# Layer 0 selective scan: VectorE runs product, product, scan, scan in each quarter

## The chip, the core and the metric

The kernel runs on one core of one Trainium2 chip, in one launch. The metric is the device time of one execution in microseconds (us), lower is better. Five engines run side by side, each with its own in-order queue: PE (TensorE, matmuls), DVE (VectorE), ACT (ScalarE), POOL (GpSimd) and SP (SyncE, which only issues DMAs here). They meet through semaphores.

## What is computed

Two "metaformer" layers over an image batch of 2 x 96 channels x 96 x 96. Layer 0 is a Mamba-like block: a 3x3 convolution gives sampling offsets, the sampled image is cut into windows, and every window is run through a selective scan in four directions with 16 states. Then come a layer norm, a gate, a projection and a small quantized MLP. Layer 1 is an attention block with an MLP. The change is in the scan of layer 0:

```
def step(hst, inputs):
    ut, dt, bt, ct = inputs
    dA = jnp.exp(dt[..., None] * A)
    hst = hst * dA + (dt * ut)[..., None] * bt[:, :, None, :]
    y = jnp.einsum('bkdn,bkn->bkd', hst, ct)
    return (hst, y)
```

So the scan needs, for each channel, state and time step, a decay `dA`, an input `dt*u*b`, a linear recurrence over time, a product with `c`, and a sum over the states.

## The kernel before

**Tiling.** Layer 0 works stripe by stripe: 2 images x 16 stripes of 6 rows (576 tokens). A stripe goes through three stages, which overlap with those of its neighbours: the front (`_l0_front`: norm, input projection, the 3x3 convolution `pc` at L551, the sampling, the scan's inputs), the scan (`_l0_scan`, L951) and the back (`_l0_back`: norm, gate, projection, MLP). While stripe n is scanned, the front of a later stripe and the back of an earlier one run beside it.

**The scan.** `_l0_scan` loops over 2 channel halves h, 2 orders o and 2 directions kk; each of these 8 sections (`_l0_section`, L992) loops over 4 groups of states, the quarters i (`quarter`, L1017), and each quarter over 2 token halves c (`unit`, L1034). A stripe is thus 32 quarters or 64 units, and the kernel has 1024 quarters or 2048 units. A tile of a unit is 128 partitions x 864 fp32. One quarter makes its decays on ACT, three instructions into one tile `dA` for both units (L1025). One unit u is then this chain:

- the spread (L1040, PE): a matmul copies the 288 values of b to 128 partitions, in PSUM tile `bp`;
- the product (L1044, DVE): `dur * bp`, in place over 864 columns of `bp`;
- the scan (L1060, DVE): the recurrence over `dA` and `bp`, into tile `h`;
- times_c (L1065, POOL): `h *= cre`;
- the states (L1077, PE): three or six matmuls fold the 16 states into the PSUM tile `y`, which gathers 32 units.

**Buffers.** `bp` has 2 buffers (the spread of unit u+2 has to wait for the scan of unit u), `dA` has 2 (the decays of quarter q+2 wait for the last scan of quarter q), `h` has 6 (the scan of unit u+6 needs the states of unit u to be done).

**Waits put on the product.** In a unit with c = 0 the product also carries the waits that the scans of the quarter would have: for the decays, and for times_c and the states of unit u-5 (`wait` at L998, called at L1050).

**What sets the order.** Nothing above is issued in the order of the loops. Every operation is recorded in a `_Plan` with an engine, a cost in us, the tiles it reads and writes and a due time. `order` (L142) then plays a list scheduler over all of layer 0: each engine takes, among the operations that could start first, the one with the earliest due time. A result is taken to reach another engine `LAG` us after its producer ends (L99: 1.5 for DVE, 1.0 for POOL, 0.6 for ACT, 0.5 for PE), and the same engine `SAME` = 0.06 us after. The list sorted by planned start is issued, and `_in_order` (L56) pins each engine to it. On the chip only this order remains, not the planned times: an engine takes its next instruction when its semaphores allow. Due times: the spread of a unit is due 60 tau before the unit (tau = 3.4 us), so that it goes first whenever it can; product and scan are due 30 tau after it, in the order product, scan, product, scan.

Of the kernel before, what the change touches and what calls it, by code (L numbers as in the profile page):

```python
# [13 lines left out]
ALU = mybir.AluOpType  # L14
# [14 lines left out]
WIN = 6  # L29
# [3 lines left out]
H2 = T // 2  # L33
NS = 16
KG = 4
NQ = 4
CB = 32
NBL = C // CB
# [50 lines left out]
class _Op:  # L89
    def __init__(self, eng, cost, run, due, tab):  # L90
        self.eng, self.cost, self.run, self.due, self.tab = eng, cost, run, due, tab
        self.deps, self.tiles, self.start, self.end = set(), [], None, None
        self.left, self.then, self.ready = 0, [], 0.0

SAME = 0.06
LAG = {"pe": 0.5, "dve": 1.5, "act": 0.6, "pool": 1.0, "sp": 1.5}  # L99


class _Plan:
# [39 lines left out]
    def order(self):  # L142

        free = {e: 0.0 for e in ("pe", "dve", "act", "pool", "sp")}
        ready = {e: [] for e in free}
        tab, wire = None, 0.0
        for n, o in enumerate(self.ops):
            o.no = n
            o.left = len(o.deps)
            for p in o.deps:  # L150
                p.then.append(o)
        for o in self.ops:
            if not o.left:
                ready[o.eng].append(o)
        left, out = {id(t): len(t.users) for o in self.ops for t in o.tiles}, []
        while len(out) < len(self.ops):
            best = None
            for e, queue in ready.items():
                pick = None
                for o in queue:  # L160
                    at = max(free[e], o.ready)
                    for t in o.tiles:
                        if t.slot is None:
                            s = t.place()
                            if s is None:
# [12 lines left out]
                if pick and (best is None or pick[1] < best[1]):  # L178
                    best = pick
            assert best, "the plan is stuck"  # L180
            _, at, o = best
            ready[o.eng].remove(o)
            cost = o.cost
            if o.tab is not None and o.tab != tab:
                tab, cost = o.tab, cost + 1.3
            for t in o.tiles:
                if t.slot is None:
                    t.slot = t.place()
                    t.slot[0] = t
                    if t.tag != "p":  # L190
                        t.queue.pop(0)
            o.start = at
            if o.eng == "sp":
                free["sp"] = at + 0.6
                wire = max(wire, at + 1.0) + cost
                o.end = wire + 2.0
            else:
                o.end = free[o.eng] = at + cost
            for p in o.then:
                p.left -= 1  # L200
                p.ready = max(p.ready, o.end + (SAME if p.eng == o.eng else LAG[p.eng]))
# [781 lines left out]
HEAD = 14 * SEQ  # L983


def _tail(py, b):

    n = T - HEAD
    return py.ap[NBL * CB :, b * n : b * n + n]


def _l0_section(k, P, S, f, first, o, h, kk, py, at, tau):  # L992


# [20 lines left out]
    dlr, dur = reps  # L1015
# [18 lines left out]
    def unit(u, i, c, cre, dA, t0):  # L1034
        toks = slice(c * H2, (c + 1) * H2)
        bp = S.tile(P.ps, [128, 1024], "bp", 2)
        ht = S.tile(P.rep, [128, NBL, H2], "h", P.nh)

        def spread():
            nc.tensor.matmul(  # L1040
                bp.ap[:, :H2], k.selb[:, kk, i, :], f.bc[o].ap[:, toks], start=True, stop=True)

        def product():
            nc.vector.tensor_tensor(  # L1044
                bp.ap[:, : NBL * H2].rearrange("p (b n) -> p b n", b=NBL)[:, ::-1],
                dur.ap[:, ::-1, toks],
                bp.ap[:, :H2].unsqueeze(1).to_broadcast([128, NBL, H2]), ALU.mult)
# [7 lines left out]
        def scan():  # L1055
            hv, dv = (v.rearrange("p b n -> p (b n)") for v in (ht.ap, dA.ap[:, c]))
            bv = bp.ap[:, : NBL * H2]
            if kk:
                hv, dv, bv = hv[:, ::-1], dv[:, ::-1], bv[:, ::-1]
            nc.vector.tensor_tensor_scan(hv, dv, bv, 0.0, ALU.mult, ALU.add)  # L1060

        S.op("dve", 2.0, scan, (dA, bp), (ht,), due=t0 + (1.35 - P.early["dve"]) * tau)

        def times_c():
            nc.gpsimd.tensor_tensor(  # L1065
                ht.ap, ht.ap, cre.ap[:, toks].unsqueeze(1).to_broadcast([128, NBL, H2]), ALU.mult)
            P.issued["pool", u] = latest()

        S.op("pool", 2.06, times_c, (cre,), (ht,), due=t0 + (2.3 - P.early["pool"]) * tau)

        def states():
            end = o == 1 and kk == 1 and i == NQ - 1

            def part(dst, v, stop):
                if o:
                    v = v.rearrange("p (w j i) -> p w i j", i=WIN, j=WIN)
                nc.tensor.matmul(dst, k.fold, v, start=False, stop=stop)  # L1077

            for blk in range(NBL):
                dst = py.ap[CB * blk : CB * blk + CB]  # L1080
                n = HEAD - H2 if c else H2
                part(dst[:, c * H2 : c * H2 + n], ht.ap[:, blk, :n], end and c == 1)
            if c:
                for blk in range(NBL):
                    part(_tail(py, blk), ht.ap[:, blk, n:], end and blk == NBL - 1)
            P.issued["pe", u] = latest()

        S.op("pe", 1.0, states, (ht,), (py,), due=t0 + (3.5 - P.early["pe"]) * tau)

    for i in range(NQ):  # L1090
        quarter(i)
# [2 lines left out]
def _layer0(k, tc, a, x, x2d):  # L1094


    nc = k.nc
    with ExitStack() as st:
        P = Ctx()
        pool = lambda name, bufs, **kw: st.enter_context(tc.tile_pool(name=name, bufs=bufs, **kw))  # L1100
# [747 lines left out]
def tile_metaformer(ctx: ExitStack, tc: tile.TileContext, a, out):  # L1848
# [100 lines left out]
```

## Time and profile before

| what | value |
|---|---|
| time, median of 3 runs (lowest, highest) | 8538.53 us (8529.44, 8542.10) |
| the profiled execution: time, span in the trace | 8525.04 us, 8523.3 us |
| layer 0 up to its last scan | 0 to about 6475 us of the span |
| busy share of the span: PE, DVE, ACT, POOL | 86%, 92%, 74%, 71% |
| one product, one scan (DVE) | 1044 ns, 1953 ns, x2048 each |
| one times_c (POOL) | 2027 ns, x2048 |
| mean granted TensorE clock | 0.911 |

The profile page gives, for one profiled execution, each engine's busy time, the costliest groups of instructions (line, engine, operation, output <- input, shapes, count, then busy us, mean ns of one, and idle us of the engine just before them with what ended most of it) and the chain of work that ended last. Queries of the same trace give the waits (who waited for whom), a timeline in order of time, and the busy time of each engine in chosen windows. A window's row reads: from:to, length, then busy us of PE, PEld (weight loads), DVE, ACT and POOL with the number of instructions, then granted clock, DMA share and GB/s.

### The profile page before, as it was taken

The page shows a single profiled execution, that of the slowest core. Times are in us where ns is not written, and L with a number is a line of the kernel's source. Part 1 is how long each engine was busy: PE and PEld are TensorE (multiplying, and loading weights), DVE is VectorE, ACT ScalarE, POOL GpSimd, SP SyncE. Part 2 cuts the span into 40 slices and gives each one's busy share as a digit, 9 for nine tenths or more (in the row PEclk, how much of TensorE's full clock was granted, in tenths as well). Part 3 has the DMA queues.
Part 4 walks back from the last instruction along what each step waited for, and adds up shares of the span by engine and source line. Part 5 has one row for each costly group of instructions (what it writes and reads, how often), then busy time and mean ns, then how long its engine had stood idle before and what let it go on. Part 6 is the DMA issues. An engine that isn't in the chain of part 4 may idle for free. (4 is left out here: it accounts for less than half of the span.)

```text
span 8523.3 us, 118902 instructions
## 1 busy us (share of the span) xinstructions
PE 7295.1 (86%) x43653; PEld 3402.1 (40%) x43653; DVE 7815.6 (92%) x5398; ACT 6339.3 (74%) x10688; POOL 6026.9 (71%) x3835
## 2 busy tenths in 40 slices
PE   7888888888888888888888888888866999989998
PEld 4443444444443444444444444443423223542245
DVE  3899999999999999999999999999996998959988
ACT  5777777777777777777777777777755886778867
POOL 4999999999999999999999999999984000110001
PEclk8899999999989888988999998989867999989999
DMA  2444444444444444444444444444442000110001
GB/s 89 141 153 148 150 152 147 148 151 144 149 146 144 151 146 152 149 150 153 146 150 151 146 145 151 146 151 150 146 143 76 3 2 14 34 48 3 2 21 32
DMA packets 339992, 985.62 MB, mean 116 GB/s; under 512 B 50152, under 2 KB 51872, under 8 KB 339104
## 3 DMA queue, kind: packets, MB, share of 16 engines
q1 hardware_dynamic: 337488, 977.74, 36.8%
q8 instruction: 347, 5.69, 0.3%
q14 instruction: 253, 2.07, 0.1%
q10 hardware_dynamic: 1904, 0.12, 0.0%
HBM read 797.19 MB, written 139.25 MB: 110 GB/s over the span
## 5 line engine op out<-in xcount | busy, mean ns | idle before, releaser
L1065 POOL TENSOR_TENSOR h<-h,cre 128x864 f32<-128x864 f32 x2048 | 4121.2, 2027 | 428.2 <-DVE h L1060 277.3
L1060 DVE TENSOR_TENSOR_SCAN h<-dA,bp 128x864 f32<-128x864 f32 x2048 | 3996.6, 1953 | 105.5 <-PE y L1077 25.5
L1025 ACT ACTIVATE dA<-dlr,A 128x576 f32<-128x576 f32 x3072 | 2155.9, 765 | 815.3 <-DVE h L1060 758.5
L1044 DVE TENSOR_TENSOR bp<-dur,bp 128x864 f32<-128x864 f32 x2048 | 2135.5, 1044 | 201.8 <-PE bp L1040 80.4
L1077 PE MATMUL y<-h,fold 128*32 128x288 f32 (+2 forms) x18432 | 1856.8, 449 | 465.3 <-POOL h L1065 444.4
L551 PE MATMUL pc<-xin,off 96*96 96x288 f32 x4608 | 1331.7, 421 | 0.1
L1077 PEld LDWEIGHTS y<-h,fold 128*32 128x32 f32 x18432 | 756.1, 117 | 1245.1 <-POOL h L1065 809.6
L1413 ACT ACTIVATE pr<-sc 128x960 f32<-128x960 f32 (+1 forms) x1080 | 954.1, 937 | 201.7 <-PE sc L1409 181.5
L1040 PE MATMUL bp<-bt,selb 128*128 128x288 bf16 x2048 | 640.9, 314 | 516.9 <-DVE h L1060 506.5
L1493 DVE TENSOR_TENSOR sums<-sums,pr 128x3840 f32<-128x3840 f32 (+1 forms) x240 | 959.0, 3996 | 56.7 <-ACT pr L1413 34.4
L1585 POOL MEMSET vch<- 96x32 f32 x16 | 2.4, 153 | 1298.1 <-DVE dist L1447 1208.1
L551 PEld LDWEIGHTS pc<-xin,off 96*96 96x96 f32 x4608 | 705.9, 165 | 505.9 <-issue 236.8
L1040 PEld LDWEIGHTS <-selb 128*128 128x128 bf16 x2048 | 201.5, 99 | 1204.1 <-DVE h L1060 930.4
L1409 PE MATMUL sc<-qH,kH 32*128 32x480 f32 (+1 forms) x3240 | 627.1, 602 | 10.1 <-DMA q<-qH 5.1
L1409 PE MATMUL sc<-q,kH 32*128 32x480 f32 (+1 forms) x1080 | 564.6, 602 | 0.0
L1475 PE MATMUL av<-pr,vT 128*32 128x480 f32 (+1 forms) x4320 | 533.2, 564 | 3.7 <-ACT av L1500 3.5
L1666 DVE SCALAR_TENSOR_TENSOR acc<-vch,lepe_w,acc 96x1152 f32<-96x1152 f32 x320 | 469.2, 1466 | 8.2 <-ACT vch L1601 0.4
L867 POOL TENSOR_TENSOR x<-x,fy 96x576 f32<-96x576 f32 x32 | 55.0, 1719 | 479.5 <-ACT fy L866 415.4
L1409 PEld LDWEIGHTS sc<-qH,kH 32*128 32x128 f32 x3240 | 218.9, 184 | 419.1 <-issue 219.9
L724 PE MATMUL pt<-xd,w_dt 96*128 96x288 f32 x768 | 290.5, 474 | 15.1 <-ACT xin L516 7.2
L743 POOL TENSOR_TENSOR e<-e,du 128x576 f32<-128x576 f32 x192 | 272.6, 1420 | 31.4 <-ACT du L739 30.9
L746 POOL TENSOR_TENSOR du<-dl,x 128x576 f32<-128x576 f32 x192 | 271.5, 1414 | 6.6
(270 smaller groups left out, 10018.1 us busy)
## 6 DMA issues: line engine op xcount, KB each, us to landing
cre<-c_d SPq DMA_DIRECT2D x1024, 288.0 KB
dur<-du_d SPq DMA_DIRECT2D x256, 864.0 KB
dlr<-dl_d SPq DMA_DIRECT2D x256, 864.0 KB
x<-xs SPq DMA_DIRECT2D x512, 72.0 KB
du_d<-du SPq DMA_DIRECT2D x128, 288.0 KB
dl_d<-dl SPq DMA_DIRECT2D x128, 288.0 KB
du_d<-du SPq DMA_DIRECT2D x128, 144.0 KB
dl_d<-dl SPq DMA_DIRECT2D x128, 144.0 KB
```

Of the source, the lines that this page charges most:

```text
L551: pe(H2, lambda: nc.tensor.matmul(pc.ap[:C, :H2], k.w_c1[:, ih, tap, oh * C : (oh + 1) * C], xin.ap[:, ih, 3 * c + dy : 3 * c + dy + 3, dx ...
L1025: nc.scalar.activation(dA.ap[:, :, blk, :], dlr.ap[:, blk, :].rearrange("p (c n) -> p c n", c=2), AF.Exp, scale=k.A[:, i, kg, h, blk : blk ...
L1040: nc.tensor.matmul(bp.ap[:, :H2], k.selb[:, kk, i, :], f.bc[o].ap[:, toks], start=True, stop=True)
L1044: nc.vector.tensor_tensor(bp.ap[:, : NBL * H2].rearrange("p (b n) -> p b n", b=NBL)[:, ::-1], dur.ap[:, ::-1, toks], bp.ap[:, :H2].unsquee ...
L1060: nc.vector.tensor_tensor_scan(hv, dv, bv, 0.0, ALU.mult, ALU.add)
L1065: nc.gpsimd.tensor_tensor(ht.ap, ht.ap, cre.ap[:, toks].unsqueeze(1).to_broadcast([128, NBL, H2]), ALU.mult)
L1077: nc.tensor.matmul(dst, k.fold, v, start=False, stop=stop)
L1409: nc.tensor.matmul(two[to // 2][:, to % 2, :n], kH[rows, k0 : k0 + 128], q, start=True, stop=True)
L1413: nc.scalar.activation(pr[:, 2 * i : 2 * i + 2, :n], two[i][:, :, :n], AF.Exp, scale=HD**-0.5)
L1475: nc.tensor.matmul((main if s < HEADS else other)[s * HD : (s + 1) * HD, :n], vT[:, blk, hd, :], pr[:, place(s, p), :n], start=at == 0, st ...
L1493: nc.vector.tensor_tensor(both, both, pr[:, :, :, :n], ALU.add)
L1666: S.op("dve", 1.43, lambda: nc.vector.scalar_tensor_tensor(acc.ap, src(), W.lw[:, t : t + 1], acc.ap, ALU.mult, ALU.add), (vch,), (acc,))
```

## The change

The spread, product, scan, times_c and states of a unit stay as they are, and so do all tiles and buffers. Four things differ:

- `rest` (scan, times_c, states) of the first unit of a quarter is recorded only after the product of the second. A pseudo tile `P.turn` is written by every product and scan, which makes the planner keep them in the order of recording: product 0, product 1, scan 0, scan 1, then the next quarter. Other VectorE work may still be planned between them.
- The planner takes the spread's result to reach VectorE 0.6 us after its end (`SOON`) instead of 1.5 us. Every other operation keeps `LAG`.
- The planner's cost of a product is 1.0 us instead of 1.03.
- Due times are the same.

```diff
@@ class _Op
-        self.left, self.then, self.ready = 0, [], 0.0
+        self.left, self.then, self.ready, self.lag = 0, [], 0.0, LAG
...
 SAME = 0.06
+SOON = {"dve": 0.6}
 LAG = {"pe": 0.5, "dve": 1.5, "act": 0.6, "pool": 1.0, "sp": 1.5}
@@ order
-                p.ready = max(p.ready, o.end + (SAME if p.eng == o.eng else LAG[p.eng]))
+                p.ready = max(p.ready, o.end + (SAME if p.eng == o.eng else o.lag[p.eng]))
@@ unit
-        S.op("pe", 0.3, spread, (f.bc[o],), (bp,), due=t0 - P.early["pe"] * tau)
-        S.op("dve", 1.03, product, (dur,), (bp,), due=t0 - P.early["dve"] * tau)
+        S.op("pe", 0.3, spread, (f.bc[o],), (bp,), due=t0 - P.early["pe"] * tau).lag = SOON
+        S.op("dve", 1.0, product, (dur,), (bp, P.turn), due=t0 - P.early["dve"] * tau)
+
+        def rest():
...
-        S.op("dve", 2.0, scan, (dA, bp), (ht,), due=t0 + (1.35 - P.early["dve"]) * tau)
+            S.op("dve", 2.0, scan, (dA, bp), (ht, P.turn), due=t0 + (1.35 - P.early["dve"]) * tau)
...
+        if c == 0:
+            P.behind = rest
+        else:
+            P.behind()
+            rest()
@@ _layer0
         S, tau = _Plan(k), 3.4
+        P.turn, P.behind = S.held(k.ident, "turn"), None
```

More of the change, by code (lines that the diff above doesn't have):

```diff
@@ L1050, in product @@
                 wait([("act", u), ("pool", free), ("pe", free)])
-        S.op("pe", 0.3, spread, (f.bc[o],), (bp,), due=t0 - P.early["pe"] * tau)
-        S.op("dve", 1.03, product, (dur,), (bp,), due=t0 - P.early["dve"] * tau)
[L1055 to L1060, printed above, removed]
@@ L1062, in unit @@
-        S.op("dve", 2.0, scan, (dA, bp), (ht,), due=t0 + (1.35 - P.early["dve"]) * tau)
[L1064 to L1083, printed above, removed]
-                for blk in range(NBL):
-                    part(_tail(py, blk), ht.ap[:, blk, n:], end and blk == NBL - 1)
-            P.issued["pe", u] = latest()
@@ L1088, in unit, with scan, times_c, states @@
-        S.op("pe", 1.0, states, (ht,), (py,), due=t0 + (3.5 - P.early["pe"]) * tau)
+        S.op("pe", 0.3, spread, (f.bc[o],), (bp,), due=t0 - P.early["pe"] * tau).lag = SOON
+        S.op("dve", 1.0, product, (dur,), (bp, P.turn), due=t0 - P.early["dve"] * tau)
+        def rest():
+            def scan():
+                hv, dv = (v.rearrange("p b n -> p (b n)") for v in (ht.ap, dA.ap[:, c]))
+                bv = bp.ap[:, : NBL * H2]
+                if kk:
+                    hv, dv, bv = hv[:, ::-1], dv[:, ::-1], bv[:, ::-1]
+                nc.vector.tensor_tensor_scan(hv, dv, bv, 0.0, ALU.mult, ALU.add)
+            S.op("dve", 2.0, scan, (dA, bp), (ht, P.turn), due=t0 + (1.35 - P.early["dve"]) * tau)
+            def times_c():
+                nc.gpsimd.tensor_tensor(
+                    ht.ap, ht.ap, cre.ap[:, toks].unsqueeze(1).to_broadcast([128, NBL, H2]), ALU.mult)
+                P.issued["pool", u] = latest()
+            S.op("pool", 2.06, times_c, (cre,), (ht,), due=t0 + (2.3 - P.early["pool"]) * tau)
+            def states():
+                end = o == 1 and kk == 1 and i == NQ - 1
+                def part(dst, v, stop):
+                    if o:
+                        v = v.rearrange("p (w j i) -> p w i j", i=WIN, j=WIN)
+                    nc.tensor.matmul(dst, k.fold, v, start=False, stop=stop)
+                for blk in range(NBL):
+                    dst = py.ap[CB * blk : CB * blk + CB]
+                    n = HEAD - H2 if c else H2
+                    part(dst[:, c * H2 : c * H2 + n], ht.ap[:, blk, :n], end and c == 1)
+                if c:
+                    for blk in range(NBL):
+                        part(_tail(py, blk), ht.ap[:, blk, n:], end and blk == NBL - 1)
+                P.issued["pe", u] = latest()
+            S.op("pe", 1.0, states, (ht,), (py,), due=t0 + (3.5 - P.early["pe"]) * tau)
```

## The prediction

> **What bounds the kernel now.** I read the page's busy shares first, then the busy time by window, then the timeline of VectorE, then its waits. The scan stage (250 to 6475 us), then the four eighths of one stripe's scan (eight quarters each) further in:
>
> ```profile
> 250.00:6475.00 6225.00, 5182.08 (x30861) 2518.45 (x30859) 5969.35 (x4217) 4659.94 (x8046) 5764.36 (x3555) 0.90 0.47 147
> ...
> 1149.00:1202.00 53.00, 41.30 (x235) 20.27 (x233) 48.05 (x34) 36.25 (x72) 51.01 (x31) 0.77 0.44 131
> 1202.00:1251.00 49.00, 36.99 (x219) 17.32 (x220) 47.29 (x35) 43.42 (x79) 47.22 (x30) 0.93 0.51 160
> 1251.00:1299.00 48.00, 40.78 (x267) 20.31 (x266) 47.52 (x35) 39.40 (x68) 47.73 (x33) 0.93 0.52 163
> 1299.00:1346.00 47.00, 45.23 (x267) 22.89 (x266) 46.46 (x33) 30.67 (x43) 37.82 (x22) 1.00 0.48 143
> ```
>
> VectorE (fifth number) is busy 96% of the stage: it is the bound. But POOL (seventh) stands at 93%, and not evenly: full in the first three windows, idle for 9 us in the fourth. There the convolution fills PE (third number), 45.2 of 47 us. So a faster VectorE soon meets POOL in one part of a stripe and PE in another. The pattern repeats every 197 us, the time of a stripe.
>
> ```profile
> 2549.81 1.95 DVE L1060 TENSOR_TENSOR_SCAN h<-dA,bp 128x864 f32<-128x864 f32 x1
> 2552.10 2.03 DVE L1044 TENSOR_TENSOR bp<-dur,bp 128x864 f32<-128x864 f32 x2 [0.34 <-PE bp L1040]
> 2554.04 3.79 DVE L1060 TENSOR_TENSOR_SCAN h<-dA,bp 128x864 f32<-128x864 f32 x2
> 2557.80 1.06 DVE L1044 TENSOR_TENSOR bp<-dur,bp 128x864 f32<-128x864 f32 x1
> 2558.90 1.95 DVE L1060 TENSOR_TENSOR_SCAN h<-dA,bp 128x864 f32<-128x864 f32 x1
> 2560.77 1.04 DVE L1044 TENSOR_TENSOR bp<-dur,bp 128x864 f32<-128x864 f32 x1
> 2561.84 1.95 DVE L1060 TENSOR_TENSOR_SCAN h<-dA,bp 128x864 f32<-128x864 f32 x1
> ```
>
> The old order already has a few pairs. Two products and two scans took 5.70 us to the next product (2552.10 to 2557.80). In the usual order a scan starts 1.07 us after its product, and the next product 1.87 us after that scan, so a quarter is 5.89.
>
> ```profile
> DVE bp L1044 <- PE bp L1040: 80.1, 79, 3.3
> DVE bp L1044 <- PE y L1077: 48.6, 30, 3.1
> DVE h L1060 <- PE y L1077: 21.7, 11, 3.6
> DVE bp L1044 <- POOL h L1065: 9.9, 22, 0.8
> ```
>
> VectorE's waits in the stage (total us, times, longest) are about 180 us, 5.7 per stripe. A stripe now is 32 x 5.89 = 188.5, plus 3.2 of other VectorE work, plus 5.6 of waits: 197.3, as seen.
>
> **Part 1, the gain.** Over all records of the stage, start to start, medians: product to its own scan 1076 ns, scan to product 1870; in the pairs product to product 949 to 972 (32 cases), scan to scan 1863 (37), and a product to a scan that is not its own about 960. A quarter goes from 2 x (1076 + 1870) = 5.89 to 960 + 960 + 1863 + 1870 = 5.65 us: 0.24 less, 7.6 per stripe, some 235 us for the 990 quarters not yet paired. The built order confirms that all 1024 quarters become product, product, scan, scan (52 groups now). What it removes is the exposed time in which a scan waits for its own product's write.
>
> The Trainium skill, "VectorE: DVE Perf Modes", section "The DRAIN you can't avoid", says that a semaphore between chained VectorE operations costs nothing and that the gap can't be skipped. By it this term would be 0, and the forecast 235 us later. The rows (1076 against 960) speak against it here, and I go by them.
>
> **Part 2, the spread loses its cover.** A spread needs the `bp` that a scan frees. From the records: scan end to weight load 0.05 us, matmul start to product start 0.33, so 0.39 at least. Before, a whole unit lay between (2.9 us). After, the spread for the first product of a quarter has the other scan (1.87), slack 1.5 us; that for the second has one product (0.96), slack 0.57. A spread behind one or two convolution matmuls (0.52 each) is just in time. In the old trace 38% of the spreads end more than 0.57 us later than they could, 18% more than 1.47, with mean excess over all spreads of 0.42 and 0.17 us.
>
> **Part 3, POOL's lead.** The built order of PE decides how late POOL may be, since PE waits for times_c in `states` and the next spread queues behind it. Before, the spread of unit j mostly stands behind the states of unit j-4, in a stripe's first part of j-5 to j-7. After, that of each quarter's first unit stands behind the states of j-3, nearly without exception. So: scan 2 of a quarter ends; its times_c ends 2.2 us later at best (POOL does the first scan's before); the states need 0.9, the spread and its way to VectorE 0.4; the product that waits for it is due 5.65 us after that scan. POOL may be late by about 2.1 us. Before, the same sum for one unit (8.85 - 1.4 - 2.07) gave 5.3, and more in the first part. POOL's own order also becomes coarser: of the 32 quarters of a stripe 18 have two or three extra operations (1.41 us each), 10 none. A quarter with two takes 4.01 + 2.82 = 6.83 us, VectorE's 5.65 + 0.1 of other work = 5.75. Adding up the surplus quarter by quarter along the built order, and charging to VectorE what goes beyond the lead, gives 13.4 us per stripe with a lead of 2.1 and 8.8 with 5.3. The same count on the old order gives 9.4 with 5.3 and 6.0 with 7, where the trace has 5.6 for all waits: it counts a little high. I take 12 us per stripe. It replaces the old 5.6.
>
> **Part 4, PE's dense stretch.** The planner now believes that VectorE waits a third of a us for each quarter's second spread (0.5 + 0.3 + 0.6 against 1.0 + 0.06), so its quarter is longer on paper and takes more of the others' work. Costing the built order by back-to-back pitches from the trace (convolution matmul 0.52, states 1.0 and 0.9, spread 0.22; it returns 5.06 us per quarter on average, as the window shows: 5182/1024), the convolution stretch, 12 quarters of a stripe, holds 6.2 us per quarter after and 5.7 before. PE thus paces these quarters: 12 x (6.2 - 5.65) = 6.6, of which about 2 lie in POOL's stalls. I take 4.5.
>
> **What costs nothing.** ACT's decays are freed by a quarter's last scan and needed 5.65 us later (5.89 before); they take 2.1, and ACT has 4.13 of work per quarter: some 1.5 us of cover, with at worst the 0.24 per quarter given back if it goes. SP: a section's last product on `dur` runs one scan earlier, so its refill is issued earlier; the DMA engines are busy 47%, and in the scan stage VectorE hardly waited for a load. The c = 0 product's waits stand now two products ahead of the first scan rather than one; behind it queues all of VectorE, which is what parts 2 and 3 price. Layer 1 is untouched.
>
> **Sum.** After: 32 x 5.65 + 3.2 + 12 + 4.5 = 200.5 us per stripe against 197.3, 3.2 more; over some 31 stripes about +100 us. From the profiled execution's 8525.0 that is 8625, and the median of the runs lies 13.5 above that execution: 8638. I forecast 8635.
>
> **Rivals.**
> 1. *The gain arrives whole*: the lateness is absorbed and waits stay 5.6 per stripe: -235, 8300. For it: PE's mean load is only 5.06 us in 5.65. Against: POOL's 5764 us of work, with any idle at all, forbid much of it.
> 2. *Part of the gain arrives*: POOL's lead suffices to average over the half stripe. The eighths of a stripe are then set by POOL's content (6.0 and 6.5 us per quarter in the built order), by PE's (6.1) and by VectorE's with some waits (5.75): 24.35 x 8 = 194.8, with 0.5 for the rest 195.3, 2.0 less than now: -60, 8480. It decides if `states` wait for POOL no oftener than now.
> 3. *Every second spread is late* (slower side, beyond my forecast): if spreads lag as in the old trace, the waits are 1024 x (0.42 + 0.17) = 604 us in place of some 100 that such lags beyond 2.5 us explain now: -235 + 504 = +270, 8805. It decides from a lag of 0.57 us on, at the second product of a quarter.
> 4. *The order is not what it says*: ruled out by the built order.
>
> **Chances.** Rival 1 0.07, rival 2 0.18, within 0.2% (17 us, about what a measurement of this kernel can tell from no change) 0.12, my forecast (8556 to about 8740) 0.46, rival 3 0.17. So faster 0.25, same 0.12, slower 0.63. The range runs from below rival 2 to about rival 3: 8420 to 8800, leaving out rival 1 and the worst of 3. The slower side's own range is 8556 to 8800.
>
> **What would show it.** Part 1: products and scans in pairs, a clean quarter at 5.65 us, VectorE's busy time some 100 us or more lower in the scan stage. Part 2: "DVE bp waits for PE bp" rising from 80 us to several hundred, mostly at second products. Part 3: PE's waits for POOL up, POOL near 100% in the first half of a stripe. Part 4: a convolution window with PE at 97% or more and VectorE idle. I would be wrong if VectorE's waits stayed under 300 us in all, or if lateness added to itself from quarter to quarter.

## The result and the profile after

The changed kernel takes 8556.08 us (median of 15 runs, 8548.25 to 8562.38), the kernel before 8536.72 (15 runs on the same chip, 8525.24 to 8542.10): a ratio of 1.0023, 95% interval 1.0015 to 1.0031. It is 19 us slower, where 8635 (+96) was forecast. The sign was right, the size five times too large. The profiled execution has a span of 8556.3 us against 8523.3, and a mean granted clock of 0.901 against 0.911.

The page's groups after (line, engine, operation, count, then busy us, mean ns of one, and idle us ahead of them):

```profile
L1062 DVE TENSOR_TENSOR_SCAN h<-dA,bp 128x864 f32<-128x864 f32 x2048 | 3880.4, 1936 | 10.7 <-PE y L1079 5.9
...
L1045 DVE TENSOR_TENSOR bp<-dur,bp 128x864 f32<-128x864 f32 x2048 | 2098.0, 1051 | 472.4 <-PE bp L1041 299.5
```

The product's row before:

```profile
L1044 DVE TENSOR_TENSOR bp<-dur,bp 128x864 f32<-128x864 f32 x2048 | 2135.5, 1044 | 201.8 <-PE bp L1040 80.4
```

Scan and product themselves hardly moved (1936 and 1051 ns, against 1953 and 1044). What grew is the idle time at the end of the product's row: VectorE stood idle 472 us ahead of products (202 before), 300 of them put down to the spread (80 before). Its timeline, where nothing disturbs it:

```profile
1298.84 2.00 DVE L1045 TENSOR_TENSOR bp<-dur,bp 128x864 f32<-128x864 f32 x2
...
1300.75 3.79 DVE L1062 TENSOR_TENSOR_SCAN h<-dA,bp 128x864 f32<-128x864 f32 x2
...
1304.46 1.04 DVE L1045 TENSOR_TENSOR bp<-dur,bp 128x864 f32<-128x864 f32 x1
```

All 1024 quarters run as pairs, and this one takes 1304.46 - 1298.84 = 5.62 us instead of 5.89. The busy time by window (from:to, length, busy us of PE, PEld, DVE, ACT, POOL, clock, DMA share, GB/s) of the scan stage, and of two eighths of one stripe:

```profile
250.00:6475.00 6225.00, 5005.02 (x30815) 2453.96 (x30812) 5810.16 (x4208) 4591.12 (x8006) 5744.62 (x3548) 0.89 0.46 148
...
1216.00:1270.00 54.00, 40.59 (x225) 18.46 (x224) 48.01 (x37) 44.07 (x81) 53.43 (x37) 0.87 0.55 176
1270.00:1316.00 46.00, 44.24 (x289) 22.86 (x287) 45.09 (x33) 36.18 (x59) 42.74 (x27) 1.00 0.48 152
```

VectorE is busy 5810 us of the stage, 159 less than before (148 less over the whole execution), and the time did not follow. The first of the two eighths tells most: POOL is full (53.4 of 54 us), VectorE waits 6 us, and the window of eight quarters is 54 us long. In the other one, the convolution's, PE has 44.2 of 46 us and VectorE still works 45.1. The waits of the stage (total us, times, longest), first after, then before:

```profile
PEld y L1079 <- POOL h L1067: 1619.6, 1263, 3.8
PE y L1079 <- POOL h L1067: 853.6, 876, 3.3
...
DVE bp L1045 <- PE bp L1041: 294.3, 462, 2.9
```

```profile
PEld y L1077 <- POOL h L1065: 802.6, 807, 4.1
...
PE y L1077 <- POOL h L1065: 440.7, 479, 3.5
```

PE's waits for times_c have doubled. How this reaches VectorE is to be seen at one place:

```profile
1262.39 4.00 POOL L1067 TENSOR_TENSOR h<-h,cre 128x864 f32<-128x864 f32 x2
...
1263.39 3.79 DVE L1062 TENSOR_TENSOR_SCAN h<-dA,bp 128x864 f32<-128x864 f32 x2
...
1264.46 1.22 PE L1079 MATMUL y<-h,fold 128*32 128x288 f32 x6 [1.56 <-POOL h L1067]
...
1265.61 1.33 PE L725 MATMUL pt<-xd,w_dt 96*128 96x288 f32 x2
...
1266.73 1.49 PE L514 MATMUL pi<-xn,in_proj 96*96 96x384 f32 x2
...
1268.15 1.01 PE L1079 MATMUL y<-h,fold 128*32 128x216 f32 x12
...
1269.09 0.30 PE L1041 MATMUL bp<-bt,selb 128*128 128x288 bf16 x1
...
1269.60 1.06 DVE L1045 TENSOR_TENSOR bp<-dur,bp 128x864 f32<-128x864 f32 x1 [2.42 <-DMA cre<-c_d]
...
1271.00 0.29 PE L1041 MATMUL bp<-bt,selb 128*128 128x288 bf16 x1
...
1271.33 1.06 DVE L1045 TENSOR_TENSOR bp<-dur,bp 128x864 f32<-128x864 f32 x1 [0.67 <-PE bp L1041]
```

The two scans end at 1265.34 and 1267.18, and each frees a buffer for a spread. But PE is behind: it has stood idle 1.56 us until POOL's times_c of an earlier unit ended (1264.41, the first of the two in the POOL row), and its order then holds those states, four matmuls of the front (mean granted clock 0.84 from 1262 to 1267, 0.66 from there to 1270) and the states of the next unit, whose own times_c had ended 1.8 us before. Only behind them comes the spread (1269.09) of the quarter's first product, which starts 2.42 us late. (The label names the load of `cre`; what starts 0.5 us ahead of the product is the spread.) Then PE does six matmuls of the front and the back, and only then the second spread; the second product is 0.67 us late. These are the two kinds of wait that took the gain back.

In all of the trace's steady part it is the spread that comes last: all but 3 of the 564 late products start within 0.21 us of their spread's end. At first products 219 of the 247 late ones, 6.4 of 7.1 us per stripe, have in the 6 us ahead of them a wait of PE for the times_c of the states that it was to do next.

**The bill.** Counted over the records of 28 steady stripes (units 192 to 1983), VectorE's waits longer than 60 ns are 6.0 us per stripe before (2.7 at first products of a quarter, 2.1 at second ones, 1.1 at scans) and 13.1 after (7.1 and 6.0). Without its waits a stripe has become 6.6 us shorter (191.5 to 184.9); the waits have become 7.1 us longer, and the stripe goes from 197.5 to 198.0 us. A clean quarter gains more, 0.27 us or some 8 us per stripe: a late product also loses the 0.1 us by which it otherwise starts ahead of the end of the instruction in front of it. Counted from start to start, the delays are 6.8 us per stripe before and about 15 after (8.0 at first products, 7.3 at second ones). Followed along the execution, after lies 16 us behind at unit 192, 29 at unit 1984, 25 at the last scan and 33 at the end: in this pair of executions 16 us come in the first three stripes, 13 in the 28 that follow; 4 are won back in the last stripe, and 8 are added behind the last scan, in work that the change does not touch.

### The profile page after: what moved, and what is told of

Read it like the earlier page. It is cut to its first block, busy times and chain, and to the rows that moved or that the text cites. A ratio compares the mean times of both kernels' runs of the same rounds, so it can differ in the third digit from the quotient of the medians.

```text
span 8556.3 us, 118999 instructions
## 1 busy us (share of the span) xinstructions
PE 7143.7 (83%) x43653; PEld 3348.8 (39%) x43653; DVE 7668.0 (90%) x5398; ACT 6275.4 (73%) x10656; POOL 6018.6 (70%) x3835
## 5 line engine op out<-in xcount | busy, mean ns | idle before, releaser
L1067 POOL TENSOR_TENSOR h<-h,cre 128x864 f32<-128x864 f32 x2048 | 4101.4, 2024 | 449.8 <-DVE h L1062 315.4
L1062 DVE TENSOR_TENSOR_SCAN h<-dA,bp 128x864 f32<-128x864 f32 x2048 | 3880.4, 1936 | 10.7 <-PE y L1079 5.9
L1079 PE MATMUL y<-h,fold 128*32 128x288 f32 (+2 forms) x18432 | 1813.6, 440 | 888.4 <-POOL h L1067 862.2
L1045 DVE TENSOR_TENSOR bp<-dur,bp 128x864 f32<-128x864 f32 x2048 | 2098.0, 1051 | 472.4 <-PE bp L1041 299.5
L725 PE MATMUL pt<-xd,w_dt 96*128 96x288 f32 x768 | 325.2, 520 | 23.1 <-ACT r L731 7.3
L730 ACT ACTIVATE e<-pt,dt_b 128x288 f32<-128x288 f32 x384 | 190.6, 496 | 204.2 <-PE pt L725 196.5
L843 ACT CAST fh<-fph 128x288 f16<-128x288 f32 x384 | 142.2, 393 | 249.7 <-PE fph L840 249.5
```

What stands on the lines that cost most here:

```text
L1045: nc.vector.tensor_tensor(bp.ap[:, : NBL * H2].rearrange("p (b n) -> p b n", b=NBL)[:, ::-1], dur.ap[:, ::-1, toks], bp.ap[:, :H2].unsquee ...
L1067: nc.gpsimd.tensor_tensor(ht.ap, ht.ap, cre.ap[:, toks].unsqueeze(1).to_broadcast([128, NBL, H2]), ALU.mult)
```

## The experiments

What I set out to tell apart: the gain is taken back (a) by POOL, whose shorter lead holds up the states and, behind them, each quarter's first spread; (b) by the second spread's short cover behind other matmuls; (c) by PE's clock; or (d) by something in the plan that has nothing to do with the order. In the lines below "fixed" is the order of after, "free" that of before. Ratios are to the kernel before, run beside each kernel on the same chip, with a 95% interval, and where two kernels are compared their ratios are subtracted (0.01 is 85 us). "Waits" are counted as in the bill, for the profiled execution.

**The plan, with the fixed order.** Three kernels move only planning figures of after:

```diff
 late_states: the states planned later behind times_c
-  S.op("pool", 2.06, times_c, ...)
+  S.op("pool", 2.06, times_c, ...).lag = {**LAG, "pe": 1.5}
 early_spread: the spread planned 0.1 us behind the scan that frees its buffer
-  s[1] + (SAME if s[2] == e else LAG[e])
+  s[1] + (SAME if s[2] == e else 0.1 if t.tag == "bp" else LAG[e])
 early_late: both
```

> The changed kernel with one planning figure different: times_c is taken to reach PE 1.5 us after its end instead of 0.5, so the states stand later in PE's order; in the built order the spread of a quarter's first unit then stands behind the states of j-4 in 43% of the quarters (j-3 in nearly all of them before). Theory A (POOL's lead: the gain is lost where a spread queues behind states that wait for POOL, at the first product of a quarter): those waits, 7.1 us per stripe, fall by some 3, so about 90 us less than the changed kernel, near 8465 us. Theory B (the second product's spread has too little cover): the waits at second products, 6.0 per stripe, are untouched, within 20 us of the changed kernel. Theory C (POOL simply has no time left): no change, within 20 us.

late_states: 8511.38 us, 0.9969 (0.9956 to 0.9981), 46 us less than after. The first three stripes are back where they were before (unit 192 at 754 us, 769 in after), but the waits of a steady stripe mostly move: 5.5 at first and 7.2 at second products, 12.6 in all. That is none of the three expectations.

> The changed kernel with one planning figure different: a freed bp buffer is taken to be known on PE 0.1 us after the scan instead of 0.5 (the trace shows 0.05), so that less PE work is placed between a scan and the spread that needs its buffer; PE's order holds 5.6 us per quarter in the convolution stretch instead of 6.2, and half of the first spreads stand behind the states of j-4 or earlier. Theory B: waits at second products fall from 6.0 to about 2 us per stripe, some 120 us less than the changed kernel, near 8435. Theory A: only the half of first spreads that got more lead gains, some 2 to 3 us per stripe, near 8475. Theory C: within 20 us of the changed kernel.

early_spread: 8525.92 us, 0.998 (0.9971 to 0.9989), 37 us less than after. Again the waits move, 3.3 at first and 9.7 at second products, 13.0 in all, and the second ones grow where theory B had them fall to 2. Alone, each figure trades one kind of wait for the other, and either is enough to bring the kernel below the kernel before.

> The changed kernel with both planning figures of early_spread and late_states (freed bp known after 0.1 us, times_c known on PE after 1.5 us); in the built order nearly all first spreads now stand behind the states of j-4 or earlier, and PE's convolution stretch holds 5.7 us per quarter. Theories A and B (lead and cover): their gains add, near 8440. Theory C (POOL's content): waits only move, as they did in late_states and early_spread, so near the better of the two, 8500 to 8520.

early_late: 8474.99 us, 0.9945 (0.9933 to 0.9957), the fastest kernel that does the reference's whole work, 67 us below after. That lies between the expectations. In the profiled execution waits are 10.4 per stripe (3.7 and 6.7) and the stripe is 195.0 us; this execution (8446 us) is the fastest of six that reach up to 8501, so these figures flatter the kernel a little. Its waits of the scan stage:

```profile
PEld L1041 <- DVE h L1062: 1023.8, 897, 4.2
...
PEld y L1079 <- POOL h L1067: 709.7, 810, 3.8
...
PE y L1079 <- POOL h L1067: 320.7, 380, 3.6
```

PE no longer waits for POOL more than before the change (709.7 and 320.7 us, against 802.6 and 440.7). Instead it stands ready with the spread and waits for the scan, as it did before the change (1023.8 us; 454.7 in after, 910.0 before). That does not hold for every spread: second products still wait 6.7 us per stripe.

**The parts of the change alone.** no_soon is after without the planning figure `SOON`; soon_before is before with `SOON` and nothing else.

```diff
 no_soon
-  S.op("pe", 0.3, spread, ...).lag = SOON
+  S.op("pe", 0.3, spread, ...)
```

> The changed kernel with the spread's result planned to reach VectorE after 1.5 us again, as before, and all else of the change kept: the order of VectorE is still product, product, scan, scan. The planned quarter grows by 0.9 us, and the built order becomes lumpier: PE's content goes from 2.9 to 7.1 us per quarter in the parts of a stripe. Theory: in the part with 7.1 PE paces VectorE, 8 x (7.1 - 5.8) = 10 us per stripe, some 250 us more than the changed kernel, near 8800; if the order within a quarter is all that matters, within 40 us of it.

> The kernel before with one part of the change alone: the planner takes the spread's result to reach VectorE 0.6 us after its end instead of 1.5; the order of products and scans is free as before. Theory A (the planning figure matters only where the spread lies close ahead of its product, which the fixed order brings): within 0.4% of before, 8500 to 8560 us, waits 5 to 8 us per stripe. Rival B (the nearer figure is a gain in itself, and the fixed order alone is what loses): 8480 us or less. Rival C (it already pairs products and takes POOL's lead): over 8570 us, and pairs in more than half of the quarters.

no_soon: 9031.73 us, 1.0586 (1.0572 to 1.0601), waits 27.2 per stripe (13.9 and 12.3). Between the freeing scan and the late spreads PE runs convolution matmuls for 25 us per stripe (2.8 in after) and states for 14.5 (9.5). The fixed order alone thus costs 500 us, and `SOON` gives nearly all of it back, about twice the 250 us that I expected. soon_before: 8606.01 us, 1.0087 (1.0073 to 1.0101), so `SOON` alone costs 74 us. It leaves the free order free (93 pairs of products in a row, 53 in before), so neither the "no effect" that I expected nor its stated rivals hold: one planning figure moves the old order, too, by more than the whole change.

**The same figures with the free order.** That called for a control: late_before and both_before are before with the figures of late_states and early_late.

> The kernel before (order of products and scans free) with the states planned 1.5 us behind times_c, as in late_states. Theory L (the plan's small figures move a kernel of this kind by some tens of us either way, whatever the order, so one plan against one plan does not price the order): 8500 to 8620 us, not the same as before within 0.1%. Theory A (late states mend POOL's short lead, which the free order does not have): within 0.15% of before, 8516 to 8542 us.

> The kernel before with both planning figures of early_late: the spread 0.1 us behind the scan, the states 1.5 us behind times_c. With soon_before and late_before it gives four plans for the free order, beside four for the fixed one (after, late_states, early_spread, early_late: 8475 to 8556 us, mean 8517). Theory A (the gain of early_late is the fixed order's, let through): 8520 us or more here. Rival (the figures are a gain for either order): below 8490 us.

late_before: 8518.48 us, 0.9981 (0.9972 to 0.9991). both_before: 8523.03 us, 0.9988 (0.9979 to 0.9997), waits 6.1 per stripe, stripe 197.2. late_before lies within the bounds of both of its expectations and tells little; both_before decides against a gain of the figures alone. The free order gains 10 to 16 us by figures that give the fixed one 46 and 67. So with both figures the fixed order is ahead by 37 us (0.9945 against 0.9988), and most of what early_late gains is its own, let through; with late states alone the two orders are 10 us apart, within their intervals. (The fixed kernels have `SOON` as well, the free ones don't, for which it is a loss; the free order with all three figures was not run.) (The expectation of light_pool_late below gives the old distance of states and times_c as 1.0 us; in the plan it is 0.5.)

**POOL's load.** Four of POOL's step operations (L744 to L747 of after) are cut from 576 to 64 columns. Nothing else moves: the order of PE, VectorE, ACT and SP stays the same to the instruction, so each pair below differs in POOL's load alone.

```diff
-  tt(e.ap, e.ap, du.ap, ALU.subtract)
+  tt(e.ap[:, :64], e.ap[:, :64], du.ap[:, :64], ALU.subtract)
   (r, w and du likewise)
```

> The kernel before, with the four POOL operations that make the scan's step sizes (24 of POOL's 41 extra operations per stripe) cut to 64 of their 576 columns; the rest of these tiles keeps what ACT wrote, so the output is another one. The order of every engine is that of the kernel before. POOL's load falls by about 24 x 1.1 = 27 us of 184 per stripe. All theories: VectorE becomes the bound nearly throughout, its waits of 5.9 us per stripe fall to about 3, near 8450.

> The changed kernel with the same four POOL operations cut to 64 columns, its order untouched; to be read against light_pool_before. Theories A and C (POOL takes the gain back): nearly the whole gain arrives, 200 to 230 us less than light_pool_before, near 8235. Theory B (second spreads, PE alone): the waits at second products stay near 6 us per stripe against 2, so only about 235 - 120 = 115 us less than light_pool_before, near 8335.

> light_pool_after (four POOL operations cut to 64 columns, so another output) with the planner told that a freed bp buffer is known on PE after 0.1 us, as in early_spread. It asks what the 7.6 us of waits per stripe are that are left with a light POOL (4.9 at second products, 2.7 at first). Theory B (second products wait because PE work was planned between the scan and the spread): the 4.9 fall to about 2, so 90 us less than light_pool_after, near 8270. Theory A or C (what is left is still POOL): within 20 us of light_pool_after, near 8360.

> light_pool_after (POOL's four step operations cut to 64 columns, so that the output is another) with the states planned 1.5 us behind times_c instead of 1.0, as in late_states. Theory A (POOL's lead and the second spread's cover are the two takers): with POOL light the lead is not short, so this gives little, 8330 to 8380 us (light_pool_after: 8360), and second products keep 4 to 6 us of waits per stripe. Rival B (late states lie between the spreads as in late_states, where second products lost 1.2 us per stripe): 8390 to 8420 us. Rival C (POOL's lead is still what is short): below 8320 us.

> light_pool_after (output another, as above) with both planning figures of early_late: the spread 0.1 us behind the scan, the states 1.5 us behind times_c. Theory A (early spread and late states help each other as they did with the full POOL, -81 us, by keeping the states from standing between a quarter's two spreads): 8270 to 8330 us, waits below 6 us per stripe, nearly the whole 235 us gain against light_pool_before. Rival B (with a light POOL the early spread loses as in light_pool_early, +92 us, whatever the states do): 8420 to 8470 us.

| plan | ratio, full POOL | light POOL: us, ratio (interval) | POOL's load is worth | waits per stripe, light: first, second products |
|---|---|---|---|---|
| before | 1 | 8480.70, 0.9933 (0.9919 to 0.9946) | 57 us | 2.4, 0.9 |
| after | 1.0023 | 8360.47, 0.9792 (0.9778 to 0.9805) | 197 us | 2.7, 4.9 |
| late_states | 0.9969 | 8444.31, 0.9895 (0.9880 to 0.9910) | 63 us | 5.9, 5.4 |
| early_spread | 0.9980 | 8452.30, 0.9915 (0.9902 to 0.9928) | 55 us | 3.3, 7.5 |
| early_late | 0.9945 | 8470.23, 0.9926 (0.9913 to 0.9940) | 16 us | 5.3, 5.4 |

In after's plan POOL's load is worth 140 us more than in before's; first-product waits fall from 7.1 to 2.7 per stripe, which is before's value. That shows (a), that POOL takes back part of the gain. That it is its lead and not a lack of time is shown by early_late, which carries the same load in a shorter stripe: with the states placed later and the spreads earlier, that load is worth 16 us, about the least that can be told from nothing here. But (a) is not all: with a light POOL the fixed order is 120 us ahead of light_pool_before, not 235. That is theory B's number; the rest stands at second products, which wait 4.9 us per stripe against 0.9, some 124 us over 31 stripes. (Part of this may go through PE's clock: in after's plan the time at half clock, of which more below, falls from 42.1 to 33.3 us per stripe when POOL is light, in before's it stays at 37.)

My own theory missed in light_pool_early, light_pool_late and light_pool_both: they are 88 to 114 us slower than light_pool_after. With POOL light, after's own plan is the best of the four, and the figures that help with a full POOL hurt. Why is seen in light_pool_early:

```profile
1197.01 0.30 PE L1041 MATMUL bp<-bt,selb 128*128 128x288 bf16 x1 [0.42 <-DVE h L1062]
...
1197.64 1.13 PE L936 MATMUL pp<-zs,w_outb 96*96 96x288 f32 x4
1198.61 1.13 PE L936 MATMUL pp<-Y,out_proj 96*96 96x288 f32 x4
...
1199.67 0.98 PE L1079 MATMUL y<-h,fold 128*32 128x216 f32 x12
1200.59 0.30 PE L1041 MATMUL bp<-bt,selb 128*128 128x288 bf16 x1
...
1200.92 1.06 DVE L1045 TENSOR_TENSOR bp<-dur,bp 128x864 f32<-128x864 f32 x1 [1.17 <-PE bp L1041]
```

The first spread runs as soon as the scan allows (1197.01); the projection's matmuls, which light_pool_after does ahead of its first spread at this place, and the states now all stand between it and the second one (1200.59). Counting what PE does from the freeing scan's end to the spread of a late second product: states take 0.4 us per stripe in light_pool_after, 5.7 in light_pool_early, 2.6 in light_pool_late and 5.8 in light_pool_both. So with a light POOL the fixed order is ahead of light_pool_before by 120 us in one plan and by 6 to 32 in the other three: that half of the 235 can arrive is shown, not that it does so whatever the plan.

**Less work for PE.** The second half of the convolution's taps is not issued; the order of all other instructions stays.

```diff
-  pe(H2, lambda: nc.tensor.matmul(pc ..., start=(ih == 0 and tap == 0), stop=(ih == 1 and tap == 8)), ...)
+  pe(H2, lambda: ih or nc.tensor.matmul(pc ..., start=(tap == 0), stop=(tap == 8)), ...)
```

> The kernel before, planned as it is, but the second 9 of the 18 matmuls of each convolution output are not issued (half of the sum is left out, so the output is another one): some 36 matmuls of 0.5 us less on PE in each stripe, about 18 of its 160 us. The order of everything else is kept. All theories: VectorE paces the convolution stretch of this kernel already (47 us for eight quarters, 5.89 each), so within 30 us of the kernel before.

> The changed kernel with the same half of the convolution left out. Part 4 of the prediction (PE paces the dense stretch, 4.5 us per stripe): some 140 us less than the changed kernel against at most 30 for half_conv_before. Theory C (POOL's content sets the stripe, PE's stretch costs only the 2 us per stripe that the trace shows as waits at second products there): 30 to 60 us less than the changed kernel.

half_conv_before: 8540.10 us, 1.0014 (1.0006 to 1.0023). half_conv_after: 8680.94 us, 1.0181 (1.0167 to 1.0194). With less to do for PE, the fixed order becomes 135 us slower, and the free one 12. My part 4 (PE's dense stretch as a taker) expected the opposite, and falls. The reason is to be seen in the convolution stretch of half_conv_after:

```profile
1295.40 2.24 PE L552 MATMUL pc<-xin,off 96*96 96x288 f32 x4
...
1299.51 0.45 PE L1041 MATMUL bp<-bt,selb 128*128 128x288 bf16 x1
...
1300.09 1.06 DVE L1045 TENSOR_TENSOR bp<-dur,bp 128x864 f32<-128x864 f32 x1 [1.56 <-PE bp L1041]
...
1303.36 1.06 DVE L1045 TENSOR_TENSOR bp<-dur,bp 128x864 f32<-128x864 f32 x1 [2.20 <-PE bp L1041]
```

Four convolution matmuls take 2.24 us here (granted clock 0.50), and in after, in the same stretch (granted clock 1.00):

```profile
1301.94 1.21 PE L552 MATMUL pc<-xin,off 96*96 96x288 f32 x4
```

The clock granted to PE is half in 71.8 us of each stripe here, 42.1 in after (36.9 in before, 64.8 in half_conv_before). Matmuls at half speed hold the spreads up: 639 of the 1792 spreads of the steady stripes start at half clock (365 in after), and the waits at their products grow from 4.8 to 10.5 us per stripe, while those at the other products go from 8.3 to 7.5. The fixed order has no cover for that; the free order's waits go from 6.0 to 7.1 only. In the clock's records its value is 1.0 or 0.5 and nothing between, in the scan stage for stretches in multiples of 3.41 us.

The Trainium skill, "TensorE: Matmul & The Clock Gate", section "Part 1: The HAM clock gate (the "warmup" mystery)", has the rate at half or full, set by how busy PE was, and at half after an idle window of about 3.4 us. Values and step agree with this trace; but PE need not idle for a whole window here. Of the 3.41 us windows of after's steady stripes that are at full clock, 142 are followed by half clock: PE's records cover 47% of them (median; nine in ten below 54%). 1137 are followed by full clock, and none of those is covered less than 52%. So in this trace the clock falls behind a window in which PE worked about half of the time or less; with half of the convolution left out there are 233 such falls.

**More work for PE.** If the clock takes much of the gain, work that keeps PE busy might pay. Each spread matmul is issued twice into the same place, in after and in light_pool_after:

```diff
   nc.tensor.matmul(bp.ap[:, :H2], k.selb[:, kk, i, :], f.bc[o].ap[:, toks], start=True, stop=True)
+  nc.tensor.matmul(bp.ap[:, :H2], k.selb[:, kk, i, :], f.bc[o].ap[:, toks], start=True, stop=True)
```

> The changed kernel with each spread's matmul issued twice (the same result, written twice): 0.12 to 0.2 us more PE work in front of each product. Theory B alone: second products wait 0.12 to 0.2 us longer each where they wait, and first ones too, 2 to 5 us per stripe, 60 to 150 us more than the changed kernel. Theory D (half of the lateness comes from stretches in which PE's clock is granted at half because PE idles): the added work keeps the clock up, the half-clock time of 42 us per stripe falls, and the time stays within 40 us of the changed kernel or falls.

> light_pool_after (output another, as above) with each spread matmul issued twice, as in spread_twice. It puts 0.22 us more on the way of each spread and keeps PE busier. Theory clock (the second products' waits are mostly spreads that run behind matmuls at half clock): low-clock time falls below 28 us per stripe (33.2 without) and second-product waits do not rise above 4.9 us per stripe, time within 30 us of 8360. Theory cover (the slack of 0.57 us is what is short, and 0.22 is taken from it): second-product waits rise by 2 to 6 us per stripe, 8420 to 8540 us.

spread_twice: 8591.33 us, 1.0071 (1.0057 to 1.0084), 41 more than after; the time at half clock falls from 42.1 to 32.3 us per stripe, and waits rise from 13.1 to 14.3. light_pool_twice: 8386.26 us, 0.9828 (0.9815 to 0.9841), 31 more than light_pool_after; half clock 33.3 to 30.9, second-product waits 4.9 as without. The 2 to 6 us more that a pure shortage of cover would have brought did not come, and the fall below 28 us of half clock that the clock theory asked for did not either. In light_pool_twice the waits at spreads that start at half clock fall (3.8 to 3.2 us per stripe) and the others rise (3.8 to 5.0); in spread_twice both rise a little. How much of the second-product waits in after is clock and how much cover is left open.

**Cover for the spread.** I tried to take the cover's shortage away: four one-bank buffers for the spread, the product written straight into `h` in SBUF, the scan in place there.

```diff
-  bp = S.tile(P.ps, [128, 1024], "bp", 2)
+  bp = S.tile(P.ps, [128, 512], "bp", 4)
...
-  nc.vector.tensor_tensor(bp.ap[...], dur.ap[...], bp.ap[...], ALU.mult)
+  nc.vector.tensor_tensor(ht.ap, dur.ap[...], bp.ap[...], ALU.mult)
   (the scan reads and writes ht)
```

> The changed kernel with the spread no longer tied to a scan: it writes a PSUM tile of one bank (4 buffers instead of 2 of two banks), the product writes straight into h in SBUF and the scan runs in place there. A spread may now run up to four units ahead, freed by a product and not by a scan, and in the built order it stands behind the states of j-5 to j-7. Theory B (late second spreads take the gain back): VectorE's waits fall from 13 us per stripe to under 5, some 250 us less than the changed kernel, near 8300, if product and scan take no longer with SBUF operands. Theory C (POOL's content): waits stay at 9 to 12 us per stripe, near 8500. If VectorE and POOL disturb each other when the scan reads two SBUF operands, the scan's 1.94 us or times_c's 2.02 us grows, and the row shows by how much.

> The kernel before with the same edit: product, scan, product, scan, and spreads free to run ahead. Theory: its waits are 6 us per stripe, of which the 2 on spreads go, and a scan still waits for its own product: 40 to 80 us less than the kernel before, near 8470. Against own_bank_after it gives the worth of the order with the spreads out of the way: 0.24 us per quarter, 235 us, if nothing else takes it.

own_bank_after: 11467.48 us, 1.3443 (1.3425 to 1.3462); own_bank_before: 11531.71, 1.3519 (1.3501 to 1.3538). The groups of own_bank_after:

```profile
L1062 DVE TENSOR_TENSOR_SCAN h<-dA,h 128x864 f32<-128x864 f32 x2048 | 6524.2, 3222 | 4.9 <-ACT dA L1026 4.9
L1067 POOL TENSOR_TENSOR h<-h,cre 128x864 f32<-128x864 f32 x2048 | 5804.2, 2853 | 588.1 <-DVE h L1062 542.1
L1045 DVE TENSOR_TENSOR h<-dur,bp 128x864 f32<-128x864 f32 x2048 | 2045.8, 1035 | 730.7 <-PE y L1079 332.3
```

The scan, which now takes both inputs from SBUF, goes from 1936 to 3222 ns, and POOL's times_c, itself unchanged, from 2024 to 2853; the product, with one input in PSUM as before, stays at 1035. Each of the two engines pays for the other: the 13 scans that meet no POOL instruction take 1944 ns (median), and the 222 times_c that meet no scan 2014. All of the expected times were missed by some 3000 us, and the experiment says nothing on cover. A third buffer of `bp` was not tried.

## Why the prediction was wrong in size

- **Part 1 was right.** A clean quarter is 5.62 us (5.65 predicted), VectorE's busy time fell by 159 us in the stage (100 or more predicted), and with both planning figures of early_late the fixed order is 37 us ahead. The rows, and not the 0 that I set beside them, were right: the stall behind an own product is real, and goes when another instruction stands between.
- **Part 3, POOL's lead, is the step that failed, in its size.** The mechanism is shown: PE's waits for POOL doubled, POOL is full in a stripe's first half, and light_pool_after returns first-product waits to before's level. But I priced it at 12 us per stripe, and first products wait 7.1 (8.0 from start to start). My count had read 9.4 for the old order, where the trace had 5.6; scaled by that ratio, its 13.4 would have been 8.0. I saw that it counted high and took hardly anything off. (That the scaled figure fits is in part luck: the 5.6 are all of VectorE's waits, of which 2.7 stand at first products.)
- **Part 4 was wrong in its place and its prices.** I costed the states at 1.0 and 0.9 us. The records show two speeds: the three matmuls of a unit's first group start side by side and once more after 267 ns in order 0, where `h` is read contiguously, and after 498 in order 1, where the same columns are read transposed (6 x 6). Half of the groups are thus much cheaper than I took them, and PE is busy 5.5 us per quarter in its dense stretch, not 6.2. The sign that I gave, PE at 97% or more and VectorE idle, did not come: in the convolution's window PE is at 96%, and VectorE works 45.1 of its 46 us. Second products wait 2.1 us per stripe in the convolution's half of a stripe, against my 4.5.
- **Part 2 I had left nearly unpriced.** Second products wait 6.0 us per stripe, spread over the whole of it: 317 of 896 are late, mostly behind convolution, transposes, projections and the MLP's matmuls, which PE was executing, not waiting in. The sign that I gave did come: of the waits labelled with the spread (80 us before, about 300 after) two thirds stand at second products. I gave it no price in the sum.
- **The sum.** A stripe takes 198.0 us, not 200.5: 2.5 less, 78 us over 31 stripes, about what the forecast was too high by (8635 against 8556). Counted from start to start, as the sum counts, first products have 8.0 us where part 3 had 12, second ones 7.3 where part 4 had 4.5 and part 2 nothing, and a clean quarter's 0.03 us take off another 1.0 (0.3 us are left over). The second products' excess thus hid most of the error in part 3. That the sign came out right is in part luck, too: a gain and a loss of some 8 us per stripe nearly cancel, 16 us of the difference come in the first three stripes, of which I had no step (late_states regains them), and one planning figure moves the result by 37 or 46 us.
- **The rivals.** The lag of the old trace (rival 3) did not carry over as it was: it would have given 8805. What I did not see at all is how much the plan itself decides. Five plans of the fixed order lie between 8475 and 9032 us, four of the free one between 8518 and 8606; the +19 us of this change compares one of each.

## What to carry to other kernels

When an engine is freed of a stall, ask which queues now have to answer sooner, and give these their lead in the same change: here the reordering lost 0.2% until its neighbours' work was planned to suit it; the spread before it or the states behind it alone made that a gain of 0.2 to 0.3%, mostly by moving waits, and both together 0.55%. Such figures suit one balance only: with a light POOL the same two made the kernel slower. Test a count of waits on the old kernel first, and scale the new figure by what that test shows. Where a list scheduler stands between the change and the chip, run the old order with the same planning figures, too, before a few tens of microseconds are put down to the order.

## What the runs showed of the hardware

- A scan on VectorE behind its own product starts 0.11 us later than behind another one (1076 against 964 ns after the product's start), and the pairs gain 0.27 us in a clean quarter. Another unit's product between the two hides it.
- Two inputs in SBUF make VectorE and POOL hold each other up: the scan 1936 to 3222 ns, times_c 2024 to 2853, a third of the kernel's time (ratio 1.3443). The Trainium skill, "SBUF — State Buffer", section "SBUF: two separate sides", states the rule, an exclusive lock that a VectorE instruction with two SBUF inputs and a GpSimd instruction take in turn. The runs agree: where a scan meets no POOL instruction it takes 1944 ns, and the 1.3 us by which the mean scan grew are less than the whole times_c of 2.0 that it can have to wait for.
- Leaving out half of the convolution's matmuls cost 135 us with the fixed order: PE's granted clock was at half for 72 us of a stripe instead of 42, and its answers came later with less to do. In after, every 3.41 us window at full clock that PE's records cover by less than 52% was followed by half clock.
- Matmuls that read 6 x 6 transposed fp32 columns run at about half the pace of contiguous ones when the granted clock is full (498 against 267 ns from a group's start to its second pass); at half clock the difference is small (522 against 480).
